# Additions moved from TensorE to VectorE, and a quarter of the long tile's one-hot matrices made by ScalarE, in a four-layer graph kernel

## The chip, the core and the metric

The kernel runs as one program on one core of a Trainium2 chip. The core has TensorE (PE, matrix products into PSUM), VectorE (DVE), ScalarE (ACT), GpSimd (POOL, which here issues gathers and scatters) and SyncE (SP, which issues the plain loads and stores). The metric is the device time of one launch in microseconds. Before the change it is 5381.86 us, the median of three runs from 5374.81 to 5388.84 us. The profiled execution spans 5376.9 us.

## What is computed

There are 16 graphs of 1024 nodes with 64 features each, and a weighted adjacency matrix for each. Four layers follow one another, each of the form x = layernorm(x + layer(x)). Cut to what matters:

```python
# layer 0: messages, a small MLP          layer 1: mean over weighted neighbours
m  = adj @ x                              x = ln(x + (adj / max(rowsum(adj), 1)) @ x)
x  = ln(x + tanh([x, m] @ W1 + b1) @ W2 + b2)

# layers 2 and 3, both on the same thinned neighbour lists
nb    = adj > 0 off the diagonal
skip  = (count + 1) // 2 where count > 10, else 1
gone  = neighbours whose rank + 1 is a multiple of skip, made symmetric
s     = sort over the kept neighbours (the node itself included) of x, per channel
agg   = 0.25 * q25(s) + 0.5 * q50(s) + 0.25 * q75(s)       # interpolated
y     = relu((x + agg) @ W1 + b1) @ W2 + b2
x     = ln(x + y * mask)
```

## The kernel before

**Tiling.** A graph's 1024 nodes are ordered by how many neighbours they keep and cut into eight tiles of 128 nodes. Each tile has a fixed list length, `SIZES = (10, 11, 13, 14, 15, 17, 19, 33)`. For the seven short tiles GpSimd gathers the neighbours' rows from a table in HBM into a ring `got_s` of `ROOM` = 64 rows (`fetch`, line 902; the gather is line 359). For the last tile, with up to 33 rows, nothing is gathered. `fill` (line 730) builds the rows on PE: for each slot i from 1 to 32, VectorE makes a one-hot matrix `hot` of 128 x 1024 by comparing `place` with i (line 750), and 24 matmuls (`pick`, line 351) multiply it with the three bf16 parts of the features. Four slots share a PSUM half `pgk`, which ScalarE copies out (`empty`, line 744) two slots later. `hot` has six buffers (`HOTS`). VectorE then sorts each list by a network of min and max, ScalarE weighs the wanted slots (line 774), and VectorE adds them up.

**Rounds.** Round k (`sort_round`, line 931) sorts layer 2 of graph k and layer 3 of graph k-2 together. While VectorE sorts, other generators are woven in: `features` of a later graph (layers 0 and 1, line 403), `lists` (neighbour lists, line 488), `ordered` (the reordering, line 635), `fill`, `weigh`, and `finish` (the MLP, line 786) for the round before. `settle` (line 368) is the layer norm, `split` cuts features into bf16 parts.

**The order.** For PE, VectorE and ScalarE the order of the instructions is written out by the program itself. `Weave` (line 840) keeps a clock that counts the planned time of VectorE's instructions alone (`Metered`, line 193: 0.13 us + size/960, or size/3840 for a 16-bit `tensor_scalar`). Each generator says by `yield u` that its next piece is due u planned microseconds later, times a pace. The order so made is fixed; on the chip every engine works through its own list and waits at semaphores. A yield is thus a distance in the order, not a delay.

**What the change touches.** In `features`, PE adds the bias (`ones_row` times `bias_rows`, line 448) and the residual (`ident` times `x_s`, line 449) into PSUM, and ScalarE copies the result to `y` (line 451); ScalarE also divides by the degree, one node tile at a time (line 475). In `finish`, PE adds `xc` and `agg` while transposing them (lines 794 and 795), adds the bias (line 809), and ScalarE multiplies by the mask (line 812). In `fill`, VectorE makes all 32 one-hot matrices.

Of the kernel before, what the change touches and what calls it, by code (L numbers as in the profile page):

```python
# [12 lines left out]
F32 = mybir.dt.float32  # L13
# [8 lines left out]
P = 128  # L22
# [7 lines left out]
HOTS = 6  # L30
ROOM = 64
LONG = 40
# [180 lines left out]
def adj_resnorm_kernel(ctx: ExitStack, tc: tile.TileContext, x, adj_t, nodemask, w01, b01, w02, b02,  # L213
# [37 lines left out]
    for t in range(NT):  # L251
        nc.vector.tensor_scalar(scaled[:, t, :], ident, to_go[:, t : t + 1], None, op0=ALU.mult)
    eps = const.tile([P, 1], F32, name="eps")
    nc.vector.memset(eps, EPS)
# [14 lines left out]

    def row(ap, name):  # L270
        return weight(ap.rearrange("(o c) -> o c", o=1), name)

    def column(ap, name):
        return weight(ap.rearrange("(c o) -> c o", o=1), name)

    w01s, b01c, w02s = weight(w01, "w01s"), column(b01, "b01c"), weight(w02, "w02s")
    mlps = [
        (weight(w21, "w21s"), column(b21, "b21c"), weight(w22, "w22s")),
        (weight(w31, "w31s"), column(b31, "b31c"), weight(w32, "w32s")),
    ]  # L280
    bias_rows = [row(b, f"bias_row{i}") for i, b in enumerate((b02, b22, b32))]
    ones_row = const.tile([1, P], F32, name="ones_row")
    nc.vector.memset(ones_row, 1.0)
    def hats(dst, pos_shape, n1, places):
# [118 lines left out]
    def features(b, e):  # L403
# [53 lines left out]
        for h in range(NH):  # L457
# [30 lines left out]
    def lists(b, e, pace):  # L488
# [69 lines left out]
        for t in range(NT + 1):  # L558
# [14 lines left out]
            yield 2.6  # L573
        yield 3

# [59 lines left out]
    def ordered(b, e, order, own):  # L635
# [41 lines left out]
        for g in reversed(range(0, NT, G)):  # L677
            pp = s.psum.tile([P, G, P], F32, name="pp", tag="s", bufs=1)
            for c in range(g, g + G):
                for c2 in range(c + 1):  # L680
                    nc.tensor.matmul(pp[:, c - g, :], steps[:, ONSET + (c - c2) * P :][:, :P], place[:, c2, :],
                                     start=c2 == 0, stop=c2 == c)
            yield 9
            dve.tensor_mul(place[:, g : g + G, :], pp, place[:, g : g + G, :])
            yield 3
# [44 lines left out]
    def fill(k):  # L730
# [6 lines left out]
        for m, b, e in members(k):  # L737
# [48 lines left out]
    def finish(b, e, layer, agg):  # L786

        xc = e.xs[layer]
        w1s, b1c, w2s = mlps[layer]
        y = s.work.tile([P, NT, C], F32, name="y_m", bufs=1)  # L790
        for h in range(NH):
            pt = s.psum.tile([P, HALF], F32, name="pt", tag="m", bufs=1)
            for q in range(G):
                nc.tensor.matmul(pt[:C, q * P : (q + 1) * P], xc[:, h * G + q, :], ident, start=True, stop=False)
                nc.tensor.matmul(pt[:C, q * P : (q + 1) * P], agg[:, h * G + q, :], ident, start=False, stop=True)
            yield 7
# [10 lines left out]
            for q in range(G):  # L807
                nc.tensor.matmul(pd[:, q, :], h_t[:, q * P : (q + 1) * P], w2s, start=True, stop=False)
                nc.tensor.matmul(pd[:, q, :], ones_row, bias_rows[1 + layer], start=False, stop=True)
            yield 9  # L810
            for t in range(h * G, (h + 1) * G):
                nc.scalar.activation(y[:, t, :], pd[:, t - h * G, :], AF.Copy, scale=e.mask[:, t : t + 1])
        yield 4
        dve.tensor_add(y, y, xc)
# [179 lines left out]

    def per_row(ap):
        t = s.work.tile([P, C], F32, name="per_row")
        nc.sync.dma_start(t, ap.rearrange("(o c) -> o c", o=1).to_broadcast([P, C]))
        return t

    def transposed(src, name):  # L1000
# [9 lines left out]
    def layer0(adj_half, x_s, x1):  # L1010
# [20 lines left out]
        nc.vector.tensor_add(y, pd, x_s)  # L1031
        nc.vector.tensor_add(y, y, per_row(b02)[:, None, :].to_broadcast([P, NT, C]))
        nc.vector.memset(x1[:, :, C : C + 1], 1.0)
# [19 lines left out]

    def mlp(xc, agg, mask, layer, dst):
        w1s, b1c, w2s = mlps[layer]
        y = s.work.tile([P, NT, C], F32, name="y")
# [9 lines left out]
        for t in range(NT):  # L1066
            nc.tensor.matmul(pd[:, t, :], h_t[:, t * P : (t + 1) * P], w2s, start=True, stop=True)
        nc.vector.tensor_add(y, pd, per_row((b22, b32)[layer])[:, None, :].to_broadcast([P, NT, C]))
        nc.vector.tensor_mul(y, y, mask[:, :, None].to_broadcast([P, NT, C]))
# [130 lines left out]
    with tc.If(nc.values_load(over_d[:, B:]) > 0):  # L1200
        with tc.For_i(0, B) as b:
            with tc.If(nc.values_load(over_d[:, ds(b, 1)]) > 0), ExitStack() as general:
# [32 lines left out]
                for layer, (xc, xn) in enumerate(((x2, x3), (x3, x1[:, :, :C]))):  # L1235
                    with tc.tile_pool(name=f"g_lists{layer}", bufs=1) as lists:
                        long_quantiles(lists, table[layer][0], idx, wts, agg)
                    with tc.tile_pool(name=f"g_dense{layer}", bufs=1) as dense:
                        dense_quantiles(dense, xc, valid, count, longest, agg)
                    mlp(xc, agg, mask, layer, xn)  # L1240
                    if layer == 0:
# [33 lines left out]
```

## Time and profile before

| Engine | busy, us | share of the span | instructions |
|---|---|---|---|
| PE (matmul) | 3746.3 | 70% | 45268 |
| PE (weight load, beside it) | 2875.6 | 53% | 45304 |
| VectorE | 4444.1 | 83% | 8819 |
| ScalarE | 2296.3 | 43% | 6214 |
| GpSimd | 3659.3 | 68% | 3228 |

| Group of instructions | count | mean, ns | busy, us |
|---|---|---|---|
| VectorE, `hot` (line 750) | 1024 | 437 | 436.5 |
| PE, bias in `finish` (line 809) | 512 records | 347 | 133.0 |
| PE, bias in `features` (line 448) | 256 records | 363 | 70.0 |
| PE, `x_s` in `features` (line 449) | 256 records | 375 | 72.3 |
| PE, `agg` transposed and added (line 795) | 512 records | 333 | 123.9 |
| ScalarE, mask (line 812) | 256 | 320 | 59.1 |
| ScalarE, degree (line 475) | 128 | 309 | 29.3 |
| ScalarE, copy of `pd` (line 451) | 32 | 376 | 12.0 |

An fp32 matmul leaves two records in the trace, so 512 records of line 809 are 256 matmuls. Matmuls overlap, so their mean duration is longer than the distance from one to the next. VectorE's instructions mostly appear under line 207, the helper that meters them; they are told apart by their tiles. Idle time of an engine is listed with what ended it ("DVE hot <- PE pgk": VectorE waited to write `hot` until PE had read an older one). A mean over the span mixes the start, the rounds and the tail; stretches of time tell them apart.

### The profile page before, as it was taken

How to read it: one execution, taken by the hardware profiler on the slowest of the kernel's cores; microseconds unless marked ns; L12 is line 12 of the kernel's file. 1: busy time of each engine (PE TensorE's matmuls, PEld its weight loads, DVE VectorE, ACT ScalarE, POOL GpSimd, SP SyncE). 2: the span in 40 equal slices, each digit the busy share in tenths (PEclk: the TensorE clock that was granted, in tenths of full speed). 3: DMA queues.
4: the chain of work that ended last, by engine and by line, in shares of the span. 5: the costliest groups of instructions: out<-in, count | busy, mean ns of one | idle time of the engine just before them, and what ended most of it. 6: DMA issues, size and time to landing. Idle time of an engine off the chain costs nothing. (4 is left out here: it accounts for less than half of the span.)

```text
span 5376.9 us, 112554 instructions
## 1 busy us (share of the span) xinstructions
PE 3746.3 (70%) x45268; PEld 2875.6 (53%) x45304; DVE 4444.1 (83%) x8819; ACT 2296.3 (43%) x6214; POOL 3659.3 (68%) x3228
## 2 busy tenths in 40 slices
PE   6888876595967769595876849688694966434452
PEld 5656655374746657363655636466473745433341
DVE  2487777989898898979889797988979789977975
ACT  3364462455445363634445353443535344222222
POOL 0335575878777777867768686776868577777662
PEclk7887787696878779787877868687797877666655
DMA  2222321222222212112221221222122121111010
GB/s 82 64 60 54 79 49 50 50 51 61 53 60 54 58 48 65 41 35 59 56 56 46 48 52 42 60 55 54 41 56 53 40 46 24 25 23 25 19 24 10
DMA packets 420186, 259.37 MB, mean 48 GB/s; under 512 B 106164, under 2 KB 368452, under 8 KB 419652
## 3 DMA queue, kind: packets, MB, share of 16 engines
q0 software_dynamic: 102400, 105.06, 10.1%
q1 hardware_dynamic: 317252, 147.02, 9.8%
q8 instruction: 356, 5.83, 0.5%
q14 instruction: 178, 1.46, 0.1%
HBM read 239.27 MB, written 12.58 MB: 47 GB/s over the span
## 5 line engine op out<-in xcount | busy, mean ns | idle before, releaser
L359 POOL DMA_INDIRECT got_s<-table,idx x2944 | 3355.2, 1140 | 1473.6 <-issue 686.4
L355 PEld LDWEIGHTS <-hot 128*128 128x128 bf16 x24576 | 881.8, 104 | 611.8 <-DVE hot L207 468.2
L522 PE MATMUL pr<-steps,near 128*128 128x512 bf16 x1500 | 435.1, 453 | 378.0 <-ACT nb_st L503 223.8
L355 PE MATMUL pgk<-x3p,hot 128*128 128x64 bf16 x12288 | 493.2, 204 | 229.0 <-DVE hot L207 203.0
L355 PE MATMUL pgk<-x2p,hot 128*128 128x64 bf16 x12288 | 478.6, 201 | 239.1 <-DVE hot L207 216.1
L744 ACT COPY got<-pgk 128x256 f32<-128x256 f32 x256 | 94.5, 369 | 1186.0 <-PE pgk L355 1175.5
L207 DVE TENSOR_TENSOR other<-got_s 128x512 f32<-128x512 f32 (+8 forms) x900 | 514.8, 584 | 90.3 <-DMA got_s<-table,idx 75.5
L207 DVE TENSOR_SCALAR hot<-place 128x1024 bf16<-128x1024 f16 x1024 | 436.5, 437 | 129.8 <-PE pgk L355 127.2
L522 PEld LDWEIGHTS <-near 128*128 128x128 f16 x1536 | 171.2, 112 | 634.8 <-issue 521.1
L207 DVE TENSOR_TENSOR got_s<-got_s 128x384 f32<-128x384 f32 (+7 forms) x918 | 490.7, 537 | 17.5
L774 ACT ACTIVATE got_s<-got_s,wts 128x64 f32<-128x64 f32 x1568 | 400.2, 338 | 221.6 <-DVE got_s L207 221.0
L609 PE MATMUL pk<-near,order 128*128 128x512 f16 x2048 | 485.2, 393 | 0.0
L464 PE MATMUL pa<-x,adj_r 128*128 128x65 f32 x2048 | 355.2, 349 | 93.4 <-DMA adj_r<-in_adj_dram 39.2
L566 PE MATMUL pv<-minus_n,takes 128*128 128x128 bf16 x1024 | 224.7, 249 | 279.0 <-DVE takes L207 278.4
L207 DVE TENSOR_TENSOR got_s<-other 128x512 f32<-128x512 f32 (+8 forms) x774 | 409.2, 541 | 8.1
L464 PEld LDWEIGHTS pa<-x,adj_r 128*128 128x128 f32 x2048 | 343.4, 264 | 107.6 <-DMA adj_r<-in_adj_dram 40.5
L566 PEld LDWEIGHTS <-takes 128*128 128x128 bf16 x1024 | 112.9, 110 | 416.7 <-DVE takes L207 318.1
L207 DVE TENSOR_TENSOR other<-other 128x128 f32<-128x128 f32 (+13 forms) x558 | 318.6, 571 | 15.1
L609 PEld LDWEIGHTS <-order 128*128 128x128 bf16 x2048 | 198.5, 101 | 242.9 <-issue 42.5
L565 PE MATMUL pv<-scaled,near 128*128 128x128 f16 x1024 | 226.2, 250 | 105.0 <-ACT near L570 93.8
L528 ACT ACTIVATE junk<-pr,nb_st 128x1024 f16<-128x1024 f32 x256 | 282.1, 1107 | 28.7 <-PE pr L522 28.6
L431 PE MATMUL px<-adj_r,x_s 128*64 128x128 f32 x2048 | 274.7, 293 | 2.1 <-ACT node_in L434 1.4
(204 smaller groups left out, 7486.6 us busy)
## 6 DMA issues: line engine op xcount, KB each, us to landing
adj_r<-in_adj_dram SPq DMA_DIRECT2D x256, 512.0 KB
got_s<-table,idx POOLq DMA_INDIRECT x2944
x_s<-in_x_dram SPq DMA_DIRECT2D x16, 256.0 KB
table<-x SPq DMA_DIRECT2D x16, 256.0 KB
x<-table SPq DMA_DIRECT2D x16, 256.0 KB
table<-x3s,rows POOLq DMA_INDIRECT x128
out_dram<-agg,out_rows POOLq DMA_INDIRECT x128
table<-no_row SPq DMA_DIRECT2D x6, 0.2 KB
```

What stands on the lines that cost most here:

```text
L207: return call(*args, **kwargs)
L355: nc.tensor.matmul(dst, hot[:, c, :], parts[:, c, q, :], start=first and c + q == 0, stop=c == NT - 1 and q == 2)
L359: nc.gpsimd.indirect_dma_start(out=dst, out_offset=None, in_=tab, in_offset=bass.IndirectOffsetOnAxis(ap=rows, axis=0))
L431: nc.tensor.matmul(px[C:, q * P : (q + 1) * P], x_s[:, jt, :], adj[t][:, jt, :], start=jt == 0, stop=jt == NT - 1)
L464: nc.tensor.matmul(pa[:, q, :], adj[i][:, jt, :], x1[:, jt, :], start=jt == 0, stop=jt == NT - 1)
L522: nc.tensor.matmul(pr[:, h * HALF : (h + 1) * HALF], near[:, c, t * P : (t + 1) * P], steps[:, ONSET + h * HALF - c * P :][:, :HALF], star ...
L528: nc.scalar.activation(junk, prs[t - 1], AF.Sign, bias=lim[:, i, t - 1 : t], scale=-1.0, accum_out=cut_at[:, i, t - 1 : t])
L565: nc.tensor.matmul(pv[:, cols], near[:, c, rows], scaled[:, c, :], start=True, stop=False)
L566: nc.tensor.matmul(pv[:, cols], takes[:, c, rows], minus_n, start=False, stop=False)
L609: nc.tensor.matmul(cols, order[:, c, t * P : (t + 1) * P], left(c, slice(h * G, (h + 1) * G)), start=c == 0, stop=c == NT - 1)
L744: nc.scalar.copy(got[:, m, waiting[0] : waiting[0] + 4, :], waiting[1])
L774: nc.scalar.activation(prods[:, m, i, :], got[:, m, slot_id, :], AF.Copy, scale=e.wts[:, t, i : i + 1])
```

## The change

Two things are exchanged. The additions of biases and residuals, the masking and the division by the degree, which PE and ScalarE did, become VectorE operations on whole blocks. In return VectorE is relieved of one of every four one-hot matrices of the long tile: ScalarE makes the matrix for slot i+2 as relu(1 - |place - (i+2)|), in two instructions, at the time of slot i. The bias rows are loaded once, spread over all partitions. Some distances in the order are altered (2.1 to 2.4, 3 to 6, 9 to 12), and `ROOM` goes from 64 to 60.

```diff
-ROOM = 64
+ROOM = 60
...
+    minus_k = const.tile([P, KW], F32, name="minus_k")
+    nc.gpsimd.iota(minus_k, pattern=[[-1, KW]], base=0, channel_multiplier=0, allow_small_or_imprecise_dtypes=True)
+    one_f = const.tile([P, 1], F32, name="one_f")
...
             for q in range(G):
-                nc.tensor.matmul(pd[:, q, :], hid_t[:, q * P : (q + 1) * P], w02s, start=True, stop=False)
-                nc.tensor.matmul(pd[:, q, :], ones_row, bias_rows[0], start=False, stop=False)
-                nc.tensor.matmul(pd[:, q, :], ident, x_s[:, h * G + q, :], start=False, stop=True)
+                nc.tensor.matmul(pd[:, q, :], hid_t[:, q * P : (q + 1) * P], w02s, start=True, stop=True)
             yield 10
-            nc.scalar.copy(y[:, h * G : (h + 1) * G], pd)
-        yield 4
+            dve.tensor_add(y[:, h * G : (h + 1) * G], pd, x_s[:, h * G : (h + 1) * G])
+        dve.tensor_add(y, y, b02r[:, None, :].to_broadcast([P, NT, C]))
...
-            yield 1
-            for q in range(G):
-                nc.scalar.activation(y[:, h * G + q, :], pa[:, q, :C], AF.Copy, scale=deg[:, 1, q : q + 1])
-        yield 5
+            dve.tensor_mul(y[:, h * G : (h + 1) * G], pa[:, :, :C], deg[:, 1, :, None].to_broadcast([P, G, C]))
...
-        yield 3
+        yield 6
         dve.tensor_scalar(own[:, :, 0], key[:, 4], 1.0, None, op0=ALU.add)
...
-            yield 9
+            yield 12
             dve.tensor_mul(place[:, g : g + G, :], pp, place[:, g : g + G, :])
...
-                hot = s.lists.tile([P, NT, P], BF, name="hot", bufs=HOTS)
-                dve.tensor_scalar(hot, e.place, float(i), None, op0=ALU.is_equal)
+                if i % 4 == 1:
+                    far = s.work.tile([P, NT, P], F16, name="far", bufs=1)
+                    nc.scalar.activation(far, e.place, AF.Abs, bias=minus_k[:, i + 2 : i + 3])
+                    by_act = s.lists.tile([P, NT, P], BF, name="hot", bufs=HOTS)
+                    nc.scalar.activation(by_act, far, AF.Relu, bias=one_f, scale=-1.0)
+                if i % 4 == 3:
+                    hot = by_act
+                else:
+                    hot = s.lists.tile([P, NT, P], BF, name="hot", bufs=HOTS)
+                    dve.tensor_scalar(hot, e.place, float(i), None, op0=ALU.is_equal)
...
-                yield 2.1
+                yield 2.4
...
         y = s.work.tile([P, NT, C], F32, name="y_m", bufs=1)
+        dve.tensor_add(agg, agg, xc)
+        yield 2
         for h in range(NH):
             pt = s.psum.tile([P, HALF], F32, name="pt", tag="m", bufs=1)
             for q in range(G):
-                nc.tensor.matmul(pt[:C, q * P : (q + 1) * P], xc[:, h * G + q, :], ident, start=True, stop=False)
-                nc.tensor.matmul(pt[:C, q * P : (q + 1) * P], agg[:, h * G + q, :], ident, start=False, stop=True)
+                nc.tensor.transpose(pt[:C, q * P : (q + 1) * P], agg[:, h * G + q, :], ident)
...
-                nc.tensor.matmul(pd[:, q, :], h_t[:, q * P : (q + 1) * P], w2s, start=True, stop=False)
-                nc.tensor.matmul(pd[:, q, :], ones_row, bias_rows[1 + layer], start=False, stop=True)
+                nc.tensor.matmul(pd[:, q, :], h_t[:, q * P : (q + 1) * P], w2s, start=True, stop=True)
             yield 9
-            for t in range(h * G, (h + 1) * G):
-                nc.scalar.activation(y[:, t, :], pd[:, t - h * G, :], AF.Copy, scale=e.mask[:, t : t + 1])
-        yield 4
+            dve.tensor_add(y[:, h * G : (h + 1) * G], pd, b2r[:, None, :].to_broadcast([P, G, C]))
+        dve.tensor_mul(y, y, e.mask[:, :, None].to_broadcast([P, NT, C]))
         dve.tensor_add(y, y, xc)
```

The fallback for graphs with longer lists (from line 983 on) takes the same bias rows; its body is not executed with these inputs.

More of the change, by code (lines that the diff above doesn't have):

```diff
@@ L252, in adj_resnorm_kernel @@
         nc.vector.tensor_scalar(scaled[:, t, :], ident, to_go[:, t : t + 1], None, op0=ALU.mult)
+    minus_k = const.tile([P, KW], F32, name="minus_k")
+    nc.gpsimd.iota(minus_k, pattern=[[-1, KW]], base=0, channel_multiplier=0, allow_small_or_imprecise_dtypes=True)
+    one_f = const.tile([P, 1], F32, name="one_f")
+    nc.vector.memset(one_f, 1.0)
     eps = const.tile([P, 1], F32, name="eps")
@@ L268, in weight, with per_row @@
         return t
-    def row(ap, name):
-        return weight(ap.rearrange("(o c) -> o c", o=1), name)
+    def per_row(ap, name):
+        t = const.tile([P, C], F32, name=name)
+        nc.sync.dma_start(t, ap.rearrange("(o c) -> o c", o=1).to_broadcast([P, C]))
+        return t
     def column(ap, name):
         return weight(ap.rearrange("(c o) -> c o", o=1), name)
-    w01s, b01c, w02s = weight(w01, "w01s"), column(b01, "b01c"), weight(w02, "w02s")
+    w01s, b01c, w02s, b02r = weight(w01, "w01s"), column(b01, "b01c"), weight(w02, "w02s"), per_row(b02, "b02r")
     mlps = [
-        (weight(w21, "w21s"), column(b21, "b21c"), weight(w22, "w22s")),
-        (weight(w31, "w31s"), column(b31, "b31c"), weight(w32, "w32s")),
-    ]
-    bias_rows = [row(b, f"bias_row{i}") for i, b in enumerate((b02, b22, b32))]
-    ones_row = const.tile([1, P], F32, name="ones_row")
-    nc.vector.memset(ones_row, 1.0)
+        (weight(w21, "w21s"), column(b21, "b21c"), weight(w22, "w22s"), per_row(b22, "b22r")),
+        (weight(w31, "w31s"), column(b31, "b31c"), weight(w32, "w32s"), per_row(b32, "b32r")),
+    ]
     def hats(dst, pos_shape, n1, places):
@@ L788, in finish @@
         xc = e.xs[layer]
-        w1s, b1c, w2s = mlps[layer]
+        w1s, b1c, w2s, b2r = mlps[layer]
         y = s.work.tile([P, NT, C], F32, name="y_m", bufs=1)
+        dve.tensor_add(agg, agg, xc)
+        yield 2
         for h in range(NH):
@@ L993, in layernorm @@
         nc.vector.tensor_mul(dst, y, st[:, 0, :, None].to_broadcast([P, NT, C]))
[L995 to L998, printed above, removed]
     def transposed(src, name):
@@ L1031, in layer0 @@
         nc.vector.tensor_add(y, pd, x_s)
-        nc.vector.tensor_add(y, y, per_row(b02)[:, None, :].to_broadcast([P, NT, C]))
+        nc.vector.tensor_add(y, y, b02r[:, None, :].to_broadcast([P, NT, C]))
         nc.vector.memset(x1[:, :, C : C + 1], 1.0)
@@ L1052, in layer1, with mlp @@
         layernorm(x2, y)
-    def mlp(xc, agg, mask, layer, dst):
-        w1s, b1c, w2s = mlps[layer]
+    def mlp(xc, agg, mask, weights, dst):
+        w1s, b1c, w2s, b2r = weights
         y = s.work.tile([P, NT, C], F32, name="y")
@@ L1067, in mlp @@
             nc.tensor.matmul(pd[:, t, :], h_t[:, t * P : (t + 1) * P], w2s, start=True, stop=True)
-        nc.vector.tensor_add(y, pd, per_row((b22, b32)[layer])[:, None, :].to_broadcast([P, NT, C]))
+        nc.vector.tensor_add(y, pd, b2r[:, None, :].to_broadcast([P, NT, C]))
         nc.vector.tensor_mul(y, y, mask[:, :, None].to_broadcast([P, NT, C]))
@@ L1239, in adj_resnorm_kernel @@
                         dense_quantiles(dense, xc, valid, count, longest, agg)
-                    mlp(xc, agg, mask, layer, xn)
+                    mlp(xc, agg, mask, mlps[layer], xn)
                     if layer == 0:
```

## The prediction

> **What bounds the kernel now.** First the page's shares of busy time: no engine is full over the whole span, so the bound has to be looked for by stages.
>
> ```profile
> PE 3746.3 (70%) x45268; PEld 2875.6 (53%) x45304; DVE 4444.1 (83%) x8819; ACT 2296.3 (43%) x6214; POOL 3659.3 (68%) x3228
> ```
>
> Then the busy times in stretches of 150 us. One round takes about 306 us: the copies of line 740 that open the fill of a round start at 1053.9 us and, five rounds later, at 2586.4 us in the timeline. Two rows are therefore one round.
>
> ```profile
> 1500.00:1650.00 150.00, 84.24 (x634) 61.41 (x634) 145.01 (x256) 76.92 (x221) 116.96 (x97) 0.70 0.25 60
> 1650.00:1800.00 150.00, 135.70 (x2190) 107.95 (x2190) 127.69 (x255) 67.38 (x174) 113.72 (x106) 0.93 0.21 48
> ```
>
> After the length come PE, PEld, DVE, ACT and POOL. The reader is to see two kinds of half round. In one VectorE (DVE) is full (145 of 150) and PE is at half. In the other, where the long tile is filled, PE is at 136 of 150, at a granted clock of 0.93, and VectorE falls to 128. So VectorE carries the time, and it loses some of it where PE is crowded. What it loses is in the list of its waits from 1000 to 4125 us, about ten rounds:
>
> ```profile
> DVE hot L207 <- PE pgk L355: 87.6, 41, 6.9
> DVE y_m L207 <- ACT y_m L812: 72.7, 9, 10.9
> DVE place L207 <- PE pp L681: 56.6, 10, 9.3
> DVE near L207 <- DMA adj_r<-in_adj_dram: 35.3, 6, 8.8
> DVE best L207 <- ACT code L620: 21.1, 12, 3.3
> ```
>
> The whole list sums to 318 us, 31 us a round. The first three rows and 11.8 us of `counted` are 229 us, 22 a round, and all come from PE being late: in the timeline before the wait of `y_m` at 2362.6 us, ScalarE had sat 14.05 us at line 744 for a pick of PE, with the four activations of line 812 queued behind it, while PE ran from 2346.7 us on with one gap, of 0.46 us. The same waits of ScalarE make up the longest row of the whole profile:
>
> ```profile
> ACT got L744 <- PE pgk L355: 1175.5, 196, 18.6
> ```
>
> GpSimd's gathers (1.14 us each, and 0.3 us between) fill about 86% of the span, and from 1000 to 4125 us GpSimd waited 120.1 us in 31 pieces for ScalarE to free the ring (`got_s` of line 774), so it follows the sorts rather than leads them.
>
> **What the Trainium skill says.** "ScalarE: Activation LUTs", section "What ACT_TABLE_LOAD costs", prices an ACTIVATE with a per-partition bias at 280 ns + 0.833 ns an element, 1133 ns for 1024; the trace agrees (1140 ns, the row of `dist` below). Its section on table sets says that abs and relu are in every set, so the new pair adds no table load; that no load stood before line 543's Abs in the trace agrees. "VectorE: DVE Perf Modes", section on mode 2×_2P, says that an fp32 `tensor_tensor` stays at one element a cycle; the trace shows 684 to 690 ns for 512 elements, from PSUM (`place`) as from SBUF. "TensorE: Matmul & The Clock Gate", in "Architectural detail", calls ScalarE's and VectorE's queues strict FIFO; the 14.05 us wait above with finished work queued behind it is that.
>
> **The change part by part.** The rows that price it:
>
> ```profile
> L207 DVE TENSOR_SCALAR hot<-place 128x1024 bf16<-128x1024 f16 x1024 | 436.5, 437 | 129.8 <-PE pgk L355 127.2 <-issue 2.4
> L207 DVE TENSOR_TENSOR got_s<-got_s 128x256 f32<-128x256 f32 x212 | 90.2, 426 | 5.8
> L207 DVE TENSOR_TENSOR y_m<-y_m,x2s 128x512 f32<-128x512 f32 x16 | 11.0, 690 | 81.9 <-ACT y_m L812 81.9
> L543 ACT ACTIVATE dist<-slot,nb_st 128x1024 f16<-128x1024 f16 x128 | 138.8, 1140 | 124.8 <-DVE nb_st L207 114.4 <-DVE takes L207 9.8
> L572 ACT ACTIVATE junk<-near 128x1024 f16<-128x1024 f16 x128 | 135.3, 1057 | 4.1
> 2348.63 0.43 PE L809 MATMUL pd<-bias_row,ones_row 1*128 1x64 f32 x2
> 2348.99 0.44 PE L808 MATMUL pd<-w22s,h_t 128*128 128x64 f32 x2
> ```
>
> *VectorE.* Out: 256 of 1024 one-hot matrices (8 of 32 in each of 32 fills), 256 x 0.437 = 112 us. In: for each of 16 batches two additions of 128x256 from PSUM, one of 128x512 and two multiplications of 128x256 by the reciprocal degree, 4 x 0.42 + 0.69 = 2.37 us, together 38 us; for each of 32 finishes two operations of 128x512 and two of 128x256, 2.22 us, together 71 us. Net: 3 us less. The engine that carries the time gets no lighter; a gain can only come out of its waits.
>
> *PE.* In the last two lines a bias matmul starts 0.36 us before the next one: that is its price on a warm clock. Out, for a round: 8 such in each of two finishes (5.8 us), 16 in the features (8 biases, 8 identity products with `x_s`, 5.8 us), and in each finish 16 accumulating transposes of about 0.22 us become 8 of 0.13 us (line 427's four took 0.53 us): 2.4 us, twice 4.8. Sum 16.4 us a round. About 11 of them (the features, and the first of the two finishes) lie in the crowded stretch; the rest lies where PE has room and is worth nothing.
>
> *ScalarE.* Out: lines 812, 475 and 451, 59 + 29 + 12 = 100 us. In: 256 pairs. Abs is 1.14 us by `dist`; Relu with a bias column lies between 1.06 (`junk`, no bias) and 1.13 (the page); I take 1.10. 256 x 2.24 = 573 us. Net +473 us, from 43% to 51%, or 36 us a round in the fill. ScalarE stood 1175 us at line 744, and each pair is queued ahead of such a wait, so most of it lies under time in which ScalarE waits anyway. Queued behind a pair are the copies out of PSUM, the layer-norm steps and the codes of the lists, on which PE and VectorE wait; each can come up to 2.2 us later.
>
> *The new wait.* A pick of matrix 4j+3 now waits for ScalarE. Its pair is issued two matrices earlier, about 4.8 planned us ahead, and takes 2.2. It is late only where ScalarE was held just before. No row of before shows this; the bounds are 0 and about 1.5 us (2.2 and a backlog of some 4 us, less 4.8) for each of some 8 pairs in the crowded stretch: 0 to 12 us a round. I take 2.5.
>
> *The ring of six.* Before, matrix i waits for the pick of i-6. Now matrix 4j+3 takes its buffer two matrices early, and counting the allocations 4j+2 waits for the pick of 4j-1: VectorE may lead PE by 3 picks, at 2.4 planned us 7.2 us, where it was 6 at 2.1, 12.6 us. PE's lateness that could hide in that lead now shows: up to 5.4 us a round lost.
>
> *The yields.* 2.1 to 2.4 spreads a fill from 73 to 82 planned us and puts some 4 us of picks beyond the crowded stretch; 9 to 12 ahead of `place` and 3 to 6 ahead of `own` let VectorE do other work in up to 57 and 12 us of waits in ten rounds. These are the same lateness of PE as above, so I count none of it again. The planner's own sum of VectorE time stays within 3 us, and a ring of 60 rows still holds 19 + 17 + 15 and then 14 + 13 + 11 + 10, as one of 64 does: no gather moves for it. Constants and their loads lie in the first microseconds beside other loads: nothing.
>
> *The ends.* Where little else runs, chains are bare and the clock is low (f32 matmuls about 0.7 us). Features lose 16 x 0.7 = 11 us of PE in two batches before VectorE is full, where 55.8 us of its waits lie on `y_x`; a finish loses 8 x 0.7 and some 4 us for the transposes, bare about twice in the tail, where `y_m` cost 42.9 us. Part of that is under the planned distances: I take 35 us for both ends.
>
> *Sum.* A round: 11 less for PE, 5.4 more for the ring, 2.5 more for late pairs: 3 us less, over 14 crowded rounds 42; with the ends 77. 5377 - 77 = **5300 us**.
>
> **The rivals.** (1) *PE's relief shows in full.* For it: 22 us a round are lost to PE, and ScalarE's idle time is ample. Then neither the ring nor the pairs cost anything, and the fill's spreading gives its 4 us: (11 + 4) x 14 + 35 = 245, or 5130 us; half of the ring's loss gives 5170. (2) *Slower: ScalarE becomes the crowded engine.* For it: it is already held in order by PE, PE is held by it in turn (`pr` waited 149.4 us for `junk` of line 528), and pairs in the fill put 36 us into a stretch where it had 67 busy of 150 and was held for most of the rest. With 12 us for pairs, 5.4 for the ring, 1 for later codes and norms, less 11: 7 us a round more, 100 in all; less 35 at the ends: 5440 us. Against it: the pairs stand ahead of the waits. (3) *No change*: loss and relief cancel, 5375 us.
>
> **How the numbers follow.** Forecast 0.41, rival 1 0.14, rival 2 0.36, no change 0.09. Faster by over 0.3% is the forecast and rival 1: 0.55; slower is rival 2: 0.36; same 0.09. The range takes all of the forecast, rival 1's softer half and rival 2 up to 40 us beyond its middle: 5170 to 5480.
>
> **What would show it.** VectorE's busy time within 20 us of 4444; ScalarE near 2770, with its wait at the `got` copies well under 1175; PE some 260 to 350 us less busy. The row of `y_m` waiting for ScalarE is gone; a row of the additions waiting for `pd` is short. The row of `hot` waiting for PE grows or holds: the ring. A long row of PE `pgk` waiting for ScalarE's `hot`, tens of us in ten rounds, is rival 2. I would be wrong if VectorE's busy time moved by more than 50 us, or if GpSimd's gathers began to hold VectorE in the middle of the span.

## The result, and the profile after

The kernel after takes **5170.31 us** (median of 4 runs, 5165.07 to 5180.50), the kernel before 5383.99 us (4 runs, 5374.81 to 5388.84). The ratio is 0.9607, with a 95% interval of 0.9587 to 0.9627: 3.9% faster. The forecast was 5300 us, 1.4% faster. The direction was right; the gain was nearly three times as large.

The shares of busy time of the kernel after, in the order PE, weight loads, VectorE, ScalarE, GpSimd:

```profile
PE 3420.0 (66%) x43512; PEld 2622.0 (51%) x43512; DVE 4472.1 (86%) x8771; ACT 2755.6 (53%) x6304; POOL 3632.1 (70%) x3229
```

PE lost 326 us and ScalarE gained 459, as worked out. VectorE has 28 us more to do, and the launch is 214 us shorter all the same: the gain came out of its waits. Two stretches of 150 us, about one round, stand for the middle of the span (length, then PE, PEld, DVE, ACT and POOL, then PE's clock, the DMA share and GB/s):

```profile
1500.00:1650.00 150.00, 88.34 (x766) 65.22 (x766) 142.06 (x247) 89.25 (x227) 120.13 (x99) 0.68 0.22 54
1650.00:1800.00 150.00, 127.49 (x1982) 99.18 (x1979) 132.92 (x264) 82.75 (x169) 114.58 (x109) 0.89 0.24 55
```

In the half round of the fill PE is at 127 of 150 us instead of 136, and VectorE at 133 instead of 128. VectorE's waits in ten rounds, from 1051 to 4007 us of the kernel after, about the fourth to the fourteenth fill (us in total, times, longest):

```profile
DVE y_m L207 <- PE pd L816: 102.8, 10, 11.4
DVE deg L207 <- PE pa L465: 14.1, 6, 3.4
DVE hot L207 <- PE pgk L358: 11.1, 6, 8.0
DVE best L207 <- ACT code L618: 5.7, 5, 1.2
```

The whole list sums to 142 us; in the stretch that the prediction took it was 318. `hot` fell from 87.6 to 11.1, and `place` (56.6), `near` (35.3) and `counted` (11.8) are gone or under 3 us. What stays is one new wait for each round, that of the first addition of `finish` for its product in `pd`. ScalarE's wait at the copies of the fill, over the whole span, has shrunk although ScalarE does more:

```profile
ACT got L742 <- PE pgk L358: 686.2, 166, 18.3
```

The groups of instructions that price the change (count, busy us, mean ns, idle time before them):

```profile
L207 DVE TENSOR_SCALAR hot<-place 128x1024 bf16<-128x1024 f16 x768 | 343.7, 452 | 37.4 <-PE pgk L358 37.0 <-issue 0.4
L207 DVE TENSOR_TENSOR y_m<-pd,b22r 128x256 f32<-128x256 f32 x32 | 13.3, 416 | 112.8 <-PE pd L816 112.8
L207 DVE TENSOR_TENSOR y_x<-y_x,b02r 128x512 f32<-128x512 f32 x16 | 11.1, 692 | 0.5
L750 ACT ACTIVATE far<-place,minus_k 128x1024 f16<-128x1024 f16 x256 | 294.5, 1150 | 2.9 <-DVE place L207 2.4
L752 ACT ACTIVATE hot<-far,one_f 128x1024 bf16<-128x1024 f16 x256 | 294.0, 1148 | 8.4
```

A pair on ScalarE takes 2.30 us (2.24 taken), the additions 0.42 and 0.69 us as taken. VectorE's row of one-hot matrices fell by 93 us (436.5 to 343.7) where 112 were counted; the 768 that remain take 452 ns each, 15 more than before. That is 19 of the 31 us between the 3 us less that were forecast for VectorE and the 28 us more that were measured.

Where in the span the time went is seen from the copies that open a fill. They cut the profiled execution into a stretch ahead of the first fill, a start (first to fifth fill), ten rounds (fifth to fifteenth) and a tail. These ten rounds begin one round later than those of the lists of waits above, so the sums differ a little. VectorE's waits are its gaps of over 0.15 us, GpSimd's idle time its gaps of over 0.4 us, both in the ten rounds. All numbers are worked out from the records of the traces, one profiled execution for each kernel; the experiments are told below. (In `before_less_pe_dist` PE's relief and the new distances stand together.)

| Kernel | start, us | ten rounds, us | tail, us | VectorE's waits in ten rounds | GpSimd idle in ten rounds | mean gather, ns |
|---|---|---|---|---|---|---|
| before | 1118 | 3139 | 886 | 346 | 221 | 1160 |
| after | 1125 | 2956 | 879 | 140 | 55 | 1136 |
| before_less_pe_3 | 1090 | 3007 | 877 | 217 | 54 | 1169 |
| before_distances_3 | 1105 | 2949 | 897 | 160 | 0 | 1179 |
| before_less_pe_dist | 1090 | 2956 | 883 | 167 | 0 | 1182 |
| after_more_pe_3 | 1157 | 3051 | 894 | 232 | 188 | 1124 |
| after_dve_hot | 1111 | 3003 | 913 | 138 | 0 | 1190 |
| after_old_distances | 1155 | 2957 | 890 | 146 | 24 | 1170 |
| after_pd_later | 1131 | 2950 | 886 | 133 | 51 | 1137 |
| before_act_hot_2 | 1137 | 3063 | 887 | 324 | 158 | 1145 |

Of the 198 us between the two profiled spans, 183 lie in the ten rounds: 313.9 us each before, 295.6 after. The start and the tail together are unchanged; 15 us lie ahead of the first fill. The rounds of the kernel before also grow along the span, from 302 to 324 us in these ten (the prediction's 306 us is of earlier ones); those of the kernel after are all between 293.9 and 296.2 us.

### The profile page after: what moved, and what is told of

Its sections match the earlier page's. It is cut to its first block, busy times and chain, and to the rows that moved or that the text cites. A ratio compares the mean times of both kernels' runs of the same rounds, so it can differ in the third digit from the quotient of the medians.

```text
span 5178.8 us, 109085 instructions
## 1 busy us (share of the span) xinstructions
PE 3420.0 (66%) x43512; PEld 2622.0 (51%) x43512; DVE 4472.1 (86%) x8771; ACT 2755.6 (53%) x6304; POOL 3632.1 (70%) x3229
## 5 line engine op out<-in xcount | busy, mean ns | idle before, releaser
L362 POOL DMA_INDIRECT got_s<-table,idx x2944 | 3320.8, 1128 | 1358.9 <-issue 675.0
L358 PEld LDWEIGHTS <-hot 128*128 128x128 bf16 x24576 | 961.9, 109 | 843.4 <-DVE hot L207 661.0
L358 PE MATMUL pgk<-x3p,hot 128*128 128x64 bf16 x12288 | 554.2, 213 | 363.1 <-DVE hot L207 328.0
L358 PE MATMUL pgk<-x2p,hot 128*128 128x64 bf16 x12288 | 512.6, 206 | 324.6 <-DVE hot L207 286.3
L520 PE MATMUL pr<-steps,near 128*128 128x512 bf16 x1536 | 421.6, 440 | 288.4 <-ACT junk L526 183.1
L207 DVE TENSOR_TENSOR got_s<-got_s 128x384 f32<-128x384 f32 (+6 forms) x918 | 491.8, 538 | 19.7
L564 PE MATMUL pv<-minus_n,takes 128*128 128x128 bf16 x1024 | 243.5, 262 | 300.5 <-DVE takes L207 299.9
L207 DVE TENSOR_SCALAR hot<-place 128x1024 bf16<-128x1024 f16 x768 | 343.7, 452 | 37.4 <-PE pgk L358 37.0
L563 PE MATMUL pv<-scaled,near 128*128 128x128 f16 x1024 | 244.9, 263 | 166.4 <-ACT near L568 165.2
L752 ACT ACTIVATE hot<-far,one_f 128x1024 bf16<-128x1024 f16 x256 | 294.0, 1148 | 8.4
```

The lines of the kernel that those rows point to most:

```text
L207: return call(*args, **kwargs)
L358: nc.tensor.matmul(dst, hot[:, c, :], parts[:, c, q, :], start=first and c + q == 0, stop=c == NT - 1 and q == 2)
L362: nc.gpsimd.indirect_dma_start(out=dst, out_offset=None, in_=tab, in_offset=bass.IndirectOffsetOnAxis(ap=rows, axis=0))
L520: nc.tensor.matmul(pr[:, h * HALF : (h + 1) * HALF], near[:, c, t * P : (t + 1) * P], steps[:, ONSET + h * HALF - c * P :][:, :HALF], star ...
L563: nc.tensor.matmul(pv[:, cols], near[:, c, rows], scaled[:, c, :], start=True, stop=False)
L564: nc.tensor.matmul(pv[:, cols], takes[:, c, rows], minus_n, start=False, stop=False)
```

## The experiments

Each ratio is to the kernel before on the same chip, with its 95% interval.

### Is PE's relief enough by itself?

The kernel before loses the matmuls that add: the biases, the residual of layer 0 and `x` in `x + agg` are left out of what it computes. Nothing takes their place, and the order is unchanged. The third bias, in `finish`, goes in the same way.

```diff
-nc.tensor.matmul(pd[:, q, :], hid_t[...], w02s, start=True, stop=False)
-nc.tensor.matmul(pd[:, q, :], ones_row, bias_rows[0], start=False, stop=False)
-nc.tensor.matmul(pd[:, q, :], ident, x_s[:, h * G + q, :], start=False, stop=True)
+nc.tensor.matmul(pd[:, q, :], hid_t[...], w02s, start=True, stop=True)
...
-nc.tensor.matmul(pt[...], xc[:, h * G + q, :], ident, start=True, stop=False)
-nc.tensor.matmul(pt[...], agg[:, h * G + q, :], ident, start=False, stop=True)
+nc.tensor.transpose(pt[...], agg[:, h * G + q, :], ident)
...
```

> The kernel before with the matmuls taken out that the change takes out of PE (the three biases, the residual of layer 0 and x in x + agg are left out of the computation), order unchanged. Where TensorE runs without stalls at issue (kernel before near 5384 us): theory PE 5180 to 5230 us, theory order 5330 to 5370, theory ScalarE's matrices 5370 to 5390. With the stalls (kernel before near 7200 us) it is expected at a ratio of 0.965 again.

Measured: 5188.76 us, 0.9639 [0.9621, 0.9657]. The three largest waits that the prediction laid to PE have at least halved (72.7, 87.6 and 56.6 us in the kernel before), here from 1050 to 4050 us:

```profile
DVE y_m L207 <- ACT y_m L808: 37.1, 8, 7.3
DVE hot L207 <- PE pgk L355: 28.1, 8, 5.5
DVE place L207 <- PE pp L679: 12.7, 8, 2.6
```

The converse puts the load back into the kernel after, with matmuls that add zero; there VectorE does its additions as well. `ROOM` is 56 here instead of 60. That moves no gather: by the code of `fetch` a round's tiles lie in the ring in two runs, of 19 + 17 + 15 = 51 rows and 14 + 13 + 11 + 10 = 48, and behind neither is there room for the next tile (65 and 67 rows in all), whether the ring has 56, 60 or 64.

```diff
-nc.tensor.matmul(pd[:, q, :], hid_t[...], w02s, start=True, stop=True)
+nc.tensor.matmul(pd[:, q, :], hid_t[...], w02s, start=True, stop=False)
+nc.tensor.matmul(pd[:, q, :], ones_row, zero[:1], start=False, stop=False)
+nc.tensor.matmul(pd[:, q, :], ident, zero, start=False, stop=True)
...
+nc.tensor.matmul(pt[...], zero, ident, start=True, stop=False)
...
```

> The changed kernel with the fp32 matmuls put back as additions of zeros, order unchanged. Without stalls at issue: theory PE 5320 to 5380 us, theory order 5190 to 5230, theory ScalarE's matrices 5170 to 5200. With them a ratio of 1.02 again.

Measured: 5334.74 us, 0.9914 [0.9886, 0.9942]: 164 of the 214 us are lost again. In both directions PE's load is worth most of the gain. In ten rounds the kernel before gained 13.2 us a round without these matmuls, and the kernel after lost 9.5 a round with them.

### Are the distances enough by themselves?

The kernel before gets the three altered distances and nothing else.

```diff
-        yield 3
+        yield 6
...
-            yield 9
+            yield 12
...
-                yield 2.1
+                yield 2.4
```

> The kernel before with the three new distances alone. Without stalls at issue: theory order 5200 to 5260 us and equally long rounds, theory PE 5340 to 5384, theory ScalarE's matrices no change. With them a ratio of 0.99 to 1.

Measured: 5190.87 us, 0.9644 [0.9624, 0.9663]. **Three numbers in the order, which remove no work from any engine, give by themselves 193 us**, as much as PE's relief (195). The waits of VectorE in ten rounds of this kernel (from 1051 to 4000 us) show what happened to the lateness of PE:

```profile
DVE other L207 <- DMA got_s<-table,idx: 143.1, 11, 18.0
DVE y_m L207 <- ACT y_m L812: 14.3, 9, 1.7
DVE ln_st_x L207 <- ACT ln_st_x L380: 9.1, 5, 2.2
DVE other L207 <- DVE got_s L207: 0.5, 1, 0.5
```

The rounds are equally long, as the expectation's theory of the order said (293.5 to 297.3 us), where PE's relief alone left them between 292 and 308. There is no row of `hot` or `place` any more. In their place VectorE waits for gathered rows. And GpSimd's own waits, in the same stretch:

```profile
POOL got_s L359 <- issue: 414.1, 1359, 0.3
POOL got_s L359 <- DMA got_s<-table,idx: 78.6, 258, 0.3
POOL got_s L359 <- DVE got_s L207: 17.1, 56, 0.3
POOL table L820 <- issue: 15.2, 50, 0.3
```

The last column is the longest of each row: 0.3 us, which stands between any two gathers. GpSimd had nothing to wait for in ten rounds. In the kernel before, from 1054 to 4115 us, the same list has rows of another kind:

```profile
POOL got_s L359 <- issue: 399.2, 1310, 0.3
POOL got_s L359 <- ACT got_s L774: 120.1, 31, 22.3
```

Both reliefs together, to see whether they add:

> The kernel before with both the matmuls taken out (biases, residual of layer 0 and x in x + agg left out of the computation) and the new distances. If the two add: 5384 - 195 - 193 = 5000 us. Theory relief: the waits for PE are already gone with one of them, and GpSimd's gathers (about 184 a round at 1.44 us and 16 scatters at 1.5, 289 us) are the floor: 5140 to 5190.

Measured: 5150.84 us, 0.9562 [0.9541, 0.9582]: 234 us, not 388. Its rounds are 295.6 us, like those of the distances alone (294.9), and GpSimd again has no idle time at all: some 200 instructions a round at 1.17 us and 0.305 us between them are 295 us. The two reliefs remove the same thing, PE's lateness, and then meet **a second bound, GpSimd's queue**.

The kernel after with the old distances:

```diff
-        yield 6
+        yield 3
...
-            yield 12
+            yield 9
...
-                yield 2.4
+                yield 2.1
```

> The changed kernel with the three old distances (2.1, 3, 9). On the chip where the kernel before takes about 5384 us: theory relief (either PE's relief or the distances are enough to empty the crowded stretch, and what remains is the next bound): 5170 to 5220 us. Theory distances (they are what keeps PE's lateness off VectorE, PE's relief matters only in their absence): 5230 to 5300. If the ring of six costs what the prediction gave it, 5.4 us a round, it shows here most: above 5250.

Measured: 5218.86 us, 0.9682 [0.9655, 0.9708], 49 us more than the kernel after. Its rounds are as short (295.7 us); by the table it loses 30 us in the start and 11 in the tail. Where PE has been relieved, the distances no longer matter to the length of the rounds.

### What do ScalarE's matrices cost and bring?

The kernel after with all 32 matrices made by VectorE:

```diff
-                if i % 4 == 3:
-                    hot = by_act
-                else:
-                    hot = s.lists.tile([P, NT, P], BF, name="hot", bufs=HOTS)
-                    dve.tensor_scalar(hot, e.place, float(i), None, op0=ALU.is_equal)
+                hot = s.lists.tile([P, NT, P], BF, name="hot", bufs=HOTS)
+                dve.tensor_scalar(hot, e.place, float(i), None, op0=ALU.is_equal)
```

> The changed kernel with all one-hot matrices by VectorE again: the additions on VectorE, the new distances and PE's relief stay, and VectorE has 112 us more to do. Theory PE: VectorE's work comes on top and nothing else changes, 5170 + 112 = 5280 us. Theory order: about the same, if the rounds stay in step (they do in the planner's order, at 291.3 planned us), 5270 to 5300. Theory ScalarE's matrices: the fill goes back to waits for PE, 5330 to 5400. With stalls at issue: 1 to 1.02.

Measured: 5253.00 us, 0.9761 [0.9743, 0.9779]. So ScalarE's matrices are worth 83 us, less than each expectation had it. In a round they are worth 4.7 us (300.3 against 295.6). VectorE's busy time in ten rounds is 50 us longer without them (2789.8 against 2739.8) and its waits are equal (138 and 140 in the table). The wait for one of the six buffers of `hot` is about the same with ScalarE's matrices (11.1 us, above) and without them, here from 1111 to 4114 us:

```profile
DVE hot L207 <- PE pgk L358: 10.0, 16, 0.8
```

And PE's weight loads waited for a matrix of ScalarE twice in the whole of the kernel after, 4.5 us together. So neither the ring nor late pairs show as waits in the kernel after.

The same matrices in the kernel before, with the new distances and the additions still on PE and ScalarE (`ROOM` is 56 here):

```diff
-ROOM = 64
+ROOM = 56
...
+                if i % 4 == 1:
...
+                    nc.scalar.activation(far, e.place, AF.Abs, bias=minus_k[:, i + 2 : i + 3])
...
+                    nc.scalar.activation(by_act, far, AF.Relu, bias=one_f, scale=-1.0)
```

> The kernel before with ScalarE's one-hot matrices and the new distances, the additions left on PE and ScalarE; VectorE has 112 us less to do. Theory relief: PE is as full as in the kernel before while VectorE's round is planned 6 us shorter, so waits for PE come back: 5180 to 5260 us. If VectorE still carried the time: 5190 - 112 = 5080. Floor of the gathers: about 5130.

Measured: 5322.05 us, 0.9874 [0.9852, 0.9897]. That is slower than every expectation. Against the distances alone (5190.87) the matrices *cost* 131 us here, although VectorE has less to do. VectorE's waits in ten rounds (from 1375 to 4438 us), then PE's:

```profile
DVE hot L207 <- PE pgk L359: 166.0, 59, 8.6
DVE y_m L207 <- ACT y_m L825: 69.3, 10, 9.3
```

```profile
PE pgk L766 <- ACT got L748: 98.6, 56, 6.8
PE pgk L359 <- ACT got L748: 55.5, 29, 4.6
```

With the distances alone VectorE's waits for picks are not in the list, and PE's two waits for the `got` copies are 13.8 and 27.6 us. These rows read as one chain: ScalarE, crowded by the pairs, frees PSUM late, PE is late with the picks, and VectorE waits for buffers of `hot`. It is the second rival's chain, in a kernel whose PE still has its whole load. The smaller ring of rows is no part of it, since 56 rows hold the tiles at the same places as 64. But with less work for VectorE the program's clock also orders everything anew, and that was not separated from ScalarE's crowding.

Put side by side, the rounds say what the matrices are worth. With PE's load in place they take 306.3 us (before_act_hot_2) or 305.1 (after_more_pe_3, where VectorE makes the additions too) with the matrices on ScalarE, and 294.9 (before_distances_3) without: the matrices cost some 10 to 11 us. With PE relieved they gain 4.7. The cost does not always show at the ring: the row of `hot` in ten rounds is 166.0 us in before_act_hot_2, but only 16.2 in after_more_pe_3, where the wait for `pd` has grown to 140.5.

### Is the new wait for `pd` a loss?

The addition from `pd` is placed 18 planned us after its matmuls instead of 9.

```diff
-            yield 9
+            yield 18
             dve.tensor_add(y[:, h * G : (h + 1) * G], pd, b2r[:, None, :].to_broadcast([P, G, C]))
```

> The changed kernel with 18 instead of 9 planned us between the matmuls of pd in the finish and VectorE's addition, where its trace shows one wait of 11 us in each round. If that wait is VectorE's own loss: 11 us a round less, 5170 - 120 = 5050 us. If it only moves to the gathers (a round of 289 us at least) or to the next thing that PE is late with: 5110 to 5170. If the longer chain delays the table of layer 3 and so its gathers: above 5170.

Measured: 5195.19 us, 0.9644 [0.9623, 0.9665]. The wait is gone, and others have come (from 1350 to 4300 us):

```profile
DVE hot L207 <- PE pgk L358: 42.1, 29, 4.7
DVE counted L207 <- PE pn L692: 32.4, 8, 7.1
DVE near L207 <- DMA adj_r<-in_adj_dram: 23.9, 9, 7.9
DVE best L207 <- ACT code L618: 22.7, 21, 2.5
```

The rounds are 295.0 us against 295.6, the start and the tail 13 us longer together. The number is that of the third case, above 5170 us, but not its reason: GpSimd's wait for the table of layer 3 fell from 17.8 to 0.6 us in ten rounds. The 102.8 us at `pd` were not time to be had: VectorE's waits move within a round whose length they don't set alone.

### Runs in which PE stands between its instructions

In three groups, ten runs in all, the kernel before takes 7145.8 to 7233.4 us instead of 5384. There PE loses time that the profile puts to nothing but issue. Of the kernel after in such a group (after_again, 7121.26 us), a row that its trace at 5170 us doesn't have:

```profile
PE pgk L358 <- issue: 982.9, 1136, 15.7
```

VectorE is busy for 63% of this span and GpSimd for 49%, so these runs are read as the edits where PE alone sets the time. The edits are those above; `before_act_hot` is that of `before_act_hot_2`.

| Kernel | us | ratio to before on the same chip |
|---|---|---|
| before_less_pe | 6908.63 | 0.9638 [0.9594, 0.9682] |
| before_less_pe_2 | 7021.25 | 0.9700 [0.9674, 0.9727] |
| after_again | 7121.26 | 0.9844 [0.9813, 0.9875] |
| before_distances | 7057.85 | 0.9849 [0.9806, 0.9893] |
| before_distances_2 | 7211.72 | 0.9974 [0.9959, 0.9989] |
| after_more_pe | 7267.29 | 1.0158 [1.0120, 1.0195] |
| after_more_pe_2 | 7401.84 | 1.0217 [1.0182, 1.0251] |
| before_act_hot | 7528.18 | 1.0512 [1.0466, 1.0557] |

> The kernel before with the matmuls taken out that the change takes out of PE, and nothing put in their place: the three biases, the residual of layer 0 and x in the sum x + agg are left out of the computation. The order and every other engine's work stay as they were. Theory PE (16.4 us of PE work a round fewer shortens the crowded stretch): most of the gain, 5384 - 150 to 200 = 5180 to 5230 us, with the waits of hot, place and y_m halved. Theory order (the stretched distances and the place of the lists beside the fill made the gain): at most a quarter, 5330 to 5370. Theory ScalarE's matrices (VectorE, relieved inside the fill, stops running into the ring): no change, 5370 to 5390.

> The kernel before with the three new distances alone (2.1 to 2.4, 3 to 6, 9 to 12). In the planner's order the lists of the next graph then end their first part 23 planned us after a round begins, in every round, where it was 10 us at round 4 and 5 us ahead of the beginning from round 7 on. Theory order: 5200 to 5260 us, and all rounds equally long. Theory PE: little, 5340 to 5384, the crowded stretch is as full as before. Theory ScalarE's matrices: no change.

> The changed kernel with as many fp32 matmuls of the same shapes put back as the change took out; they add zeros. The order stays that of the changed kernel. Theory PE: back to 5320 to 5380 us. Theory order: 5190 to 5230, since the order is what keeps PE's work apart. Theory ScalarE's matrices: 5170 to 5200.

> The kernel before with ScalarE's one-hot matrices and the new distances; the additions stay on PE and ScalarE (ring of 56 rows, which packs alike). VectorE has 112 us less work than before. Theory PE: PE stays crowded, so VectorE's relief turns into waits: 5300 to 5380. Theory order or ScalarE's matrices: the waits go as in the changed kernel and the 109 us of additions are not on VectorE: 5060 to 5120, which would beat both kernels.

> The changed kernel once more, beside the kernel before on the same chip. In the first group the kernel before took 7161 us, with TensorE standing at issue between matmuls for about 1.4 us at a time, on another chip than the 5384 us. If this group meets TensorE without those stalls: ratio 0.96 and about 5170 us. If it meets them: every theory leaves the ratio open, since TensorE then carries the time.

> The kernel before with the matmuls taken out that the change takes out of PE (the three biases, the residual of layer 0 and x in x + agg are left out of the computation), order unchanged, again. Without stalls at issue: theory PE 5180 to 5230 us, theory order 5330 to 5370, theory ScalarE's matrices 5370 to 5390.

> The kernel before with the three new distances alone, again. Without stalls at issue: theory order 5200 to 5260 us and equally long rounds, theory PE 5340 to 5384, theory ScalarE's matrices no change.

> The changed kernel with the fp32 matmuls put back as additions of zeros, order unchanged, again. Without stalls at issue: theory PE 5320 to 5380 us, theory order 5190 to 5230, theory ScalarE's matrices 5170 to 5200.

The table is in the order of the ratio. Less PE work gains 3 to 3.6% here too, the distances far less (0.3 and 1.5%), and the kernel after with PE's load put back is slower than the kernel before: what the change has beyond PE's relief is worth nothing there, and ScalarE's matrices in the kernel before cost 5.1%. The whole change keeps 1.6% of its 3.9%.

### Is GpSimd's queue the limit of the kernel after?

Both kernels gather one row more for each short tile, 7 in a round, to a place that already holds it.

```diff
             for m, b, e in members(k):
...
                     gather(got[:, m, i, :], table[m][b % 3], e.idx[:, t, i - 1 : i])
+            m, b, e = members(k)[0]
+            gather(got[:, m, 1, :], table[m][b % 3], e.idx[:, t, :1])
```

> The kernel after, with one gather more for each short tile (slot 1 of its first member is gathered a second time, to the same place; 7 more in a round). Theory (GpSimd's queue is what the kernel after runs into): in ten rounds of the kernel after GpSimd has 2007 instructions, 2298 us busy and 0.305 us between two of them, 2910 of 2956 us; 4 to 5 us a round are spare. Seven more at 1.14 + 0.305 us are 10.1 us a round: rounds of 301 to 306 us instead of 295.6, over 14 rounds 75 to 145 us more: 5245 to 5315 us. Rival (VectorE's own work bounds the rounds, GpSimd only follows): 5170 to 5190 us.

> The kernel before with the same seven gathers more in a round. Theory: in ten of its rounds (314 us each) GpSimd stood idle for 221 us in 35 pieces, 22 us a round, so 10.1 us of gathers fit in: 5385 to 5430 us, less than half of what they cost the kernel after. Rival (a gather more costs its time wherever it is put): 14 times 10.1, 5525 us. Second rival (GpSimd only follows): 5385 us here and nothing in the kernel after either.

Measured: 7084.85 us, 0.9909 [0.9877, 0.9941], for the kernel after, and 7269.11 us, 1.0159 [1.0125, 1.0193], for the kernel before. Both ran in a group of the kind just told (kernel before: 7145.8 us), where GpSimd stood idle for 1286 and 1319 us in ten rounds. The expectations were for rounds in which it has 5 or 22 us to spare, so **the question stays open for the kernel after**: that GpSimd bounds before_distances_3, before_less_pe_dist and after_dve_hot is seen in its having no idle time for ten rounds, least plainly in the last, where VectorE waited 19.8 us for gathers against 143.1 in before_distances_3; that it also sets the kernel after's 295.6 us, where it is idle for 55 us in ten rounds and VectorE waits for 140, was not shown.

## Why the prediction was right in direction and wrong in size

**What bounds the kernel.** Right: VectorE carried the time and lost it to PE being late. Of the 229 us that the prediction laid to PE in ten rounds, `hot`, `place` and `counted` fell from 156 to 14; the wait of `y_m` stayed in another form. Neither sign of being wrong came: VectorE's busy time moved by 28 us, and in the kernel after it waited 0.4 us for gathers in ten rounds. What the prediction put aside was GpSimd ("it follows the sorts rather than leads them"). That was so before. But with 221 us idle in ten rounds GpSimd left about 22 us a round to gain, and before_distances_3 and before_less_pe_dist, which gain 19.0 and 18.3, have none of it left.

**PE.** The 11 us a round are near what the matmuls' removal alone gave in the rounds (13.2), and PE's fall of 326 us lies in the 260 to 350 named.

**The ring and the late pairs: the step that failed.** 5.4 and 2.5 us a round were charged and took 7.9 of the 11 away. For the ring the prediction's "up to 5.4" went into the sum as if it were the cost. Measured, the row of `hot` did not grow or hold; it fell from 87.6 to 11.1 us in ten rounds, against 10.0 in after_dve_hot without ScalarE's matrices. Late pairs measured 4.5 us in the whole span, all at PE's weight loads. So both terms were near their lower bound, 0, and these matrices bring 4.7 us a round instead of costing 7.9. The reasoning took PE's lateness of before, which was to hide in the ring's lead, and charged it to a kernel that has had that lateness taken away: a charge and a relief of the same wait were sized apart. With PE's load in place the matrices do cost, some 10 to 11 us a round (before_act_hot_2, after_more_pe_3), though not always at the ring.

**VectorE nets to nothing: nearly right in sum, wrong in meaning.** 28 us more instead of 3 less. But the additions moved onto VectorE did not lengthen its rounds. On one way through the runs the 18.3 us a round are 13.2 for PE (before_less_pe_3), 0.4 for the additions on VectorE, the distances and all else but the matrices (from there to after_dve_hot, 300.7 to 300.3, while VectorE's waits in ten rounds fell from 217 to 138 us), and 4.7 for ScalarE's matrices. It is not the only way: the distances alone give 19.0, and the parts don't add.

**The yields, counted at nothing.** The argument, that they treat the same lateness as PE's relief, holds: with PE relieved, the old distances have rounds of the same length, and the two reliefs don't add. But it was not seen that the distances alone would remove nearly all of that lateness (193 us), nor that they are worth 49 us beside PE's relief, of which the table shows 41 in the start and the tail.

**The ends.** 35 us were forecast; 15 came, all ahead of the first fill, where the prediction looked for 11 from the features. The price of 0.7 us for a matmul at the low clock was its duration; from one to the next it is 0.62 us at the tail's end (5351 to 5354 us). before_less_pe_3 gained the same 15 us, 28 in the start and 9 in the tail; the kernel after loses the 37 again. In the start after_dve_hot is 14 us shorter than after, which would fit the pairs, but in the tail it is 34 us longer. The rest was not separated.

**ScalarE** rose by 459 us (473 forecast) and its wait at the `got` copies fell from 1175 to 686 us: right.

**The wait for `pd`** was to be short and is 102.8 us in ten rounds, longer than the `y_m` wait it replaced (72.7). Taking it away gained nothing (after_pd_later).

**The rivals.** Rival 1, PE's relief in full, was the right one in its reason. That its variant with half the ring's loss, 5170 us, meets the number is luck: it has half a charge for the ring, of which no sign was found, 35 us for the ends, where 15 came, and nothing for what the matrices bring. Rival 2 failed for this kernel; its chain is what before_act_hot_2 seems to show, where the matrices moved without PE's relief.

## What to carry to other kernels

When an edit takes work off a late engine and another edit adds a dependence on it, don't price the second by the lateness in the profile before: that lateness is what the first removes. Where several waits of the bounding engine have one cause, compare the next engine's idle time in the same stretch: here GpSimd's 22 us a round told roughly how far any relief went (at most 19.0). And try distances in the order by themselves: three of them gave the kernel before 3.6% with no instruction changed.

## What the runs showed of the hardware

**A gather takes longer beside a VectorE operation with two inputs.** In the ten rounds of the kernel before, grouped by what VectorE did while GpSimd issued a gather: 953 ns on average where VectorE was idle for most of it (194 gathers), 954 ns inside its MAX8 (55), 1252 ns where tensor_tensor filled over 80% of it (1035). In the kernel after: 946, 943 and 1210 ns. Beside a tensor_scalar, which reads one tensor, it is between them (1082 ns before, 63 gathers), so two inputs are not the whole of it. The Trainium skill, "SBUF — State Buffer", section "SBUF: two separate sides", says that a VectorE operation with two SBUF inputs and a GpSimd operation that reads SBUF exclude one another at a shared port. The longer gathers beside tensor_tensor agree with it, if a gather counts as such an operation; no run took the sorts away to show it. The prediction had used a mean of 1.14 us as if it were fixed; by kernel it lies between 1124 and 1190 ns. If the grouping tells the cause, GpSimd's bound of about 295 us a round is itself partly made by the sorts.

**PE can stand between its instructions with no releaser in the trace.** In three groups of runs the kernel before took 7146 to 7233 us. In after_again PE stood so 1136 times before the picks, 0.87 us on average; its busy time for the same instructions was 3914.5 us against 3420.0 elsewhere, and its granted clock 0.681 against 0.756. VectorE's busy time was nearly the same (4485.6 and 4472.1 us). Why this is so is open. Whether it belongs to the chip is open too: the chips of these groups bear the numbers 7, 9 and 8, and in a later group on a chip of number 7 the kernel before took 5384.77 us.
